# First loads of a decoder layer over two queues, with the other loads behind the first layernorm, and four pieces of work in other places

## The chip, the cores and the metric

One core of one Trainium2 chip runs the kernel. The core has TensorE (PE, matmuls; its weight loads are listed as PEld), VectorE (DVE), ScalarE (ACT), GpSimd (POOL) and SyncE (SP, which here only issues transfers), an on-chip memory of 128 partitions, and matmul accumulators (PSUM) in banks of 512 fp32 numbers a partition. Transfers (DMAs) are issued by SP, ACT or POOL, each on a queue of its own, and carried out by 16 DMA engines. The metric is the device time of one execution in microseconds (us); less is better. All numbers are fp32.

## The reference

A pre-layernorm decoder layer on x (4 batches, 1024 tokens, 512 features), with 16 heads of 32, and a context of 4 x 1024 x 384:

```
def attn(x):                                  # phase 0: gated self-attention
    aperture, expression = sigmoid(x @ Wa + ba), sigmoid(x @ We + be)   # (B, T, 16): the gates
    inner, outer, v = heads(x @ Wi), heads(x @ Wo), heads(x @ Wv)
    a = softmax(inner @ outer.T / sqrt(32)) * aperture[q] * expression[k]
    a = a / (a.sum(-1) + 1e-8)
    c = (a @ v) * sigmoid(iv_p)
    c = rotate(c, angle = pi * sigmoid(beta_p)) * sigmoid(ov_p) * tanh(chi)   # a rotation per head
    return merge(c) @ Wout
def xattn(x, ctx):                            # phase 1: cross-attention
    q, k, v = heads(x @ Wq + bq), heads(ctx @ Wk + bk), heads(ctx @ Wv + bv)
    return merge(softmax(clip(q @ k.T * 32**-0.5)) @ v) @ Wo + bo
def ffn(x):                                   # 64 small networks of 16 hidden units each
    s = x @ Win + bin_                        # (B, T, 64)
    g = (relu(s[..., None] * W1 + b1) * W2).sum(-1) + b2
    return g @ Wout + bout
x = x + attn(layernorm(x)); x = x + xattn(layernorm(x), ctx); return x + ffn(layernorm(x))
```

## The kernel before

**Units of work.** The time is spent in `moderate_path`. There are eight units u: phase 0 (self-attention) for batches 0 to 3, then phase 1 (cross-attention) for batches 0 to 3. A unit has two halves (hf) of 512 query tokens, each half 4 head groups (g) times 8 key tiles (kt), which is 32 steps. A step (`step`, L667) makes the scores of four heads for 128 keys (`scores`: 16 matmul records on PE at L557, two exponentials of 128x1024 on ACT at L562, sums of them on DVE, tile `es`, and in phase 0 `eg`), and then the products with the values of the step before (`times`, L584; L592 for sums of the heads that DVE leaves to PE).

**An order written out by hand.** All five engines are scheduled by hand: each engine runs its instructions in the order in which this program writes them. `pre(u)` holds what a unit needs before its attention: loads of x, layernorm (`ln`, DVE), transposes, projections to k, q and v (all matmuls of a projection are at L87; `evacuate` copies a bank to SBUF, on DVE before the first attention and on ACT after), and in phase 0 the gates (`gates`, `gates_t`). `post(u, hf)` holds what follows: output projection (`o`), layernorm, and in phase 1 the feed-forward: `s` (`inputs`), 17 pieces `h` (`hidden`: one ACT activation and one DVE sum each), `out`. `first` (L1000) runs `pre(0)` and parts of `pre(1)` before the first attention. After that `run(attention(u, hf), beside(u, hf))` deals out the pieces of `beside` among the 32 steps, in proportion to a number of matmul groups that each piece is given; pieces with 0 go along. `weave` mixes two lists evenly. PE has two banks for all this (`bank`, L80).

**Loads.** x0, the first half of batch 0, is one DMA of 1 MB on SP (L134). The rest of `first` goes on SP in order: the key weights Wo in four quarters (`by_quarters`, L89: a quarter is 256 KB, its rows taken as four blocks of 32), the second half of x, Wi and Wv in quarters. ACT issues wae (Wa and We, eight DMAs of 8 KB) and nbae (the gates' biases, eight small DMAs). POOL issues the biases bqk, bvT, bo_bc, bout_bc, the feed-forward's win in quarters, and then, as nothing holds it up, the first 26 DMAs of `load_networks`. A tile framework gives each DMA one of eight semaphores in turn, so a DMA's issue also waits until the one eight DMAs earlier on its kind of queue (SP and ACT together) has landed.

**The gates.** `gates(hf)` multiplies the normalized tokens with wae (L454), takes Exp with nbae on ACT (L460, after `negate` has negated nbae on DVE), adds 1 (tile gi), stores the aperture rows to DRAM (iap_d, L463) and reads them back in another layout (iap, L466). The read-back waits on SP for the four stores. `gates_t(hf)` transposes gi on PE and takes reciprocals on DVE into sw.

**The rotation.** `load_wout` loads Wout, rotj (the rotation's signs) and hp (four numbers a head) late in `first`. `rotations`, the first piece beside the first attention half, computes sigmoids, tanh and the sine and cosine on ACT (Exp, Tanh, Sin) and DVE, and from them four 128x128 matrices rot (L179, L180); `rotate(c)` then multiplies Wout by them on PE, and the product goes to DRAM (wout_d, L190).

**Sums of a head group.** After its eighth key tile a group's sums are copied on ACT (L601, L603, L615), stored to DRAM (`add_up`, L620, L625), read back in another layout (cs, L626, L630), divided on DVE (`divide`, L638) and spread again (L654, L658). DVE comes to `divide` two steps after `add_up`, whether cs has landed or not.

Of the kernel before, what the change touches and what calls it, by code (L numbers as in the profile page):

```python
# [63 lines left out]
def moderate_path(tc: tile.TileContext, a: dict, out: bass.AP, flag: bass.AP):  # L64
    nc = tc.nc
    x = a["x"]
    with ExitStack() as st:
# [21 lines left out]
        def by_quarters(dma, to, w):  # L89

            for c in range(NC):
                dma(to[:, c, :], w.rearrange("(q c i) f -> c q i f", c=NC, i=NB)[c])
# [28 lines left out]
        def load_w(which):  # L121
            w = wp.tile([P, NC, D], F32, tag="w", name="w")
            if which == "o0":
                nc.sync.dma_start(w, wout_d)
            else:
                src, n = W_IN[which]
                if which in ("q0", "k0", "v0", "q1"):
                    by_quarters(nc.sync.dma_start, w, src)
                else:
                    nc.sync.dma_start(w[:, 0:n, :], src.rearrange("(c p) f -> p c f", p=P))  # L130
            return w

        x0 = p2.tile([P, 4, D], F32, tag="inT", name="xin")
        nc.sync.dma_start(x0, x[0].rearrange("(t p) d -> p t d", p=P)[:, 0:4, :])  # L134
        wae = const.tile([P, NC, 2 * H], F32, name="wae")
        by_quarters(nc.scalar.dma_start, wae[:, :, 0:H], a["attn_Wa"])
        by_quarters(nc.scalar.dma_start, wae[:, :, H:], a["attn_We"])

        nbae = const.tile([P, 1], F32, name="nbae")
        for t in range(4):  # L140
            for i, k in enumerate(("attn_ba", "attn_be")):
                nc.scalar.dma_start(nbae[t * 2 * H + i * H : t * 2 * H + (i + 1) * H, :], a[k].unsqueeze(1))
# [8 lines left out]
        def load_wout():  # L151
            raw.append(wp.tile([P, NC, D], F32, tag="w", name="w"))
            nc.sync.dma_start(raw[0], a["attn_Wout"].rearrange("(c p) f -> p c f", p=P))
            nc.sync.dma_start(rotj, a["rotj"])
            nc.sync.dma_start(hp, a["headp"])

        rot = p2.tile([P, NC, P], F32, tag="r2", name="rot")

        def rotations():

            sg = p1.tile([P, 3, NC], F32, name="sg")
            nc.scalar.activation(sg, hp[:, 0:3, :], AF.Exp, scale=-1.0)
            nc.vector.tensor_scalar(sg, sg, 1.0, None, ALU.add)
            nc.vector.reciprocal(sg, sg)
            gain = p1.tile([P, NC], F32, name="gain")
# [8 lines left out]
            cs = p1.tile([P, 2, NC], F32, name="cs")  # L174
            nc.scalar.activation(cs, ang, AF.Sin, scale=math.pi)
# [19 lines left out]
        for k in range(2):  # L195
            nc.gpsimd.dma_start(
                bqk[k * 2 * DH : (k + 1) * 2 * DH], a["bqk"].rearrange("p w (c k) -> p w c k", k=2)[:, :, :, k]
            )

        def broadcast(name, v):  # L200
            t = const.tile([P, D], F32, name=name)
            nc.gpsimd.dma_start(t, v.partition_broadcast(P))
            return t

        bvT = const.tile([P, NC], F32, name="bvT")
        nc.gpsimd.dma_start(bvT, a["xattn_bv"].rearrange("(c p) -> p c", p=P))
        bo_bc = broadcast("bo_bc", a["xattn_bo"])
        bout_bc = broadcast("bout_bc", a["ffn_bout"])
# [17 lines left out]
        by_quarters(nc.gpsimd.dma_start, win, a["ffn_Win"])  # L226
# [112 lines left out]
        def pre(u):  # L339
# [31 lines left out]
            def ln(hf):  # L371
# [11 lines left out]
                def root():  # L383
                    res["rs"] = rsqrt(res["mv"], 4)
# [63 lines left out]
            def gates(hf):  # L448
                def f():
# [19 lines left out]
                    me["gi", hf] = gi  # L469
                return f  # L470

            def gates_t(hf):
                def f():
# [456 lines left out]
        def one(f):  # L930
            return [[(0, f)]]
# [7 lines left out]

        def beside(u, hf):  # L940
# [3 lines left out]
            if u + 1 == n:  # L944
# [7 lines left out]
                out += last["tr"] + weave(last["b"], pause(2)) + last["s"] + weave(last["h"][0:8], pause(14))  # L952
                last["h"] = last["h"][8:]
# [5 lines left out]
            if u + 1 < B:  # L959
                if hf == 0:  # L960
# [3 lines left out]
                    else:  # L964
                        out = one(rotations) + one(fold_bv) + x[1] + k[0][0:1] + [rotate(c) for c in range(NC)]
# [14 lines left out]
            if hf == 0:  # L980
                out = ahead(u + 1, "v") + last["wo"] + p["ctx"][1] + end(k[0] + v[0][0:1]) + last["load"] + v[0][1:2]
                out += last["o"] + weave(last["ln"], v[0][2:])
                if "s" in last:
                    out += last["xT"] + weave(last["b"], k[1][0:2]) + last["tr"] + k[1][2:3] + last["s"] + k[1][3:]
                    held.append(last)
                else:
                    out += k[1]
                return out + xT[0] + v[1][0:2] + tr[0]
# [702 lines left out]
```

## Time and profile before

| | us |
|---|---|
| three runs | 2254.61, 2254.63, 2257.43 |
| median | 2254.63 |
| the profiled execution, its own time | 2255.34 |
| its span in the profile | 2253.5 |
| PE busy | 2192.8 |
| DVE, ACT, POOL busy | 1572.1, 1238.2, 142.9 |
| mean granted clock of PE | 0.994 |
| first matmul (the transposes of x0, L311) | 13.29 |
| first matmul of the key projection | 20.09 |
| first gates' matmul | 40.37 |
| first scores | 113.26 |

The profile is that of one execution, and times inside it count from the span's start. Its own time is the span plus 1.84 us around it. An engine's busy time is the time in which it works on an instruction; waiting and issuing of DMAs are not counted. A row of the timeline has start, length, engine, line, operation, tiles (out<-in), shape and number, and in brackets the idle time of the engine before it and what ended that. SPq, ACTq are the sequencers of SP and ACT, with their DMA issues. The granted clock is that share of TensorE's full clock which it was allowed.

### The profile page before, as it was taken

The page shows a single profiled execution, that of the slowest core. Times are in us where ns is not written, and L with a number is a line of the kernel's source. Part 1 is how long each engine was busy: PE and PEld are TensorE (multiplying, and loading weights), DVE is VectorE, ACT ScalarE, POOL GpSimd, SP SyncE. Part 2 cuts the span into 40 slices and gives each one's busy share as a digit, 9 for nine tenths or more (in the row PEclk, how much of TensorE's full clock was granted, in tenths as well). Part 3 has the DMA queues.
Part 4 walks back from the last instruction along what each step waited for, and adds up shares of the span by engine and source line. Part 5 has one row for each costly group of instructions (what it writes and reads, how often), then busy time and mean ns, then how long its engine had stood idle before and what let it go on. Part 6 is the DMA issues. An engine that isn't in the chain of part 4 may idle for free.

```text
span 2253.5 us, 52768 instructions
## 1 busy us (share of the span) xinstructions
PE 2192.8 (97%) x22590; PEld 552.6 (25%) x22590; DVE 1572.1 (70%) x2498; ACT 1238.2 (55%) x1488; POOL 142.9 (6%) x144
## 2 busy tenths in 40 slices
PE   6999999999999999999999999999999999999995
PEld 2322222222222222222222222222222222222222
DVE  4368776697767957577686666877777776856476
ACT  0055545555455554555656565565756566577673
POOL 4000011000000000000000000101000010101010
PEclk9999999999999999999999999999999999999998
DMA  4422223122231221211413032311223142213131
GB/s 126 108 90 50 69 85 106 36 78 69 87 103 34 80 67 45 80 43 42 118 36 106 26 86 63 109 49 46 74 77 105 44 104 68 58 40 89 47 86 40
DMA packets 153289, 161.71 MB, mean 72 GB/s; under 512 B 46186, under 2 KB 91882, under 8 KB 151892
## 3 DMA queue, kind: packets, MB, share of 16 engines
q1 hardware_dynamic: 149588, 157.19, 24.3%
q8 instruction: 179, 2.93, 0.6%
q0 software_dynamic: 2144, 0.98, 0.3%
q10 hardware_dynamic: 1312, 0.07, 0.1%
q14 instruction: 66, 0.54, 0.1%
HBM read 115.40 MB, written 42.74 MB: 70 GB/s over the span
## 4 chain that ended last, share of the span: by engine, by line
PE 84%; DVE 7%; ACT 4%; DMA 2%; issue 2%; SPq 0%; DVEq 0%; ACTq 0%
PE f L87 32%; PE s L557 22%; PE av L584 18%; PE sm L592 6%; DVE es L570 4%; ACT e L562 3%; PE sm L614 3%; DVE g L847 1%; DMA w<-in_attn_Wo 1%; ACT hid L841 1%; PE f L858 1%; PE f L824 1%; DMA rec_d<-rec 0%; DVE xT L304 0%; DMA wae<-in_attn_Wa 0%
## 5 line engine op out<-in xcount | busy, mean ns | idle before, releaser
L562 ACT ACTIVATE e<-s 128x1024 f32<-128x1024 f32 x1024 | 994.0, 1022 | 730.2 <-PE s L557 541.0
L570 DVE TENSOR_TENSOR es<-es,e 128x1024 f32<-128x1024 f32 x534 | 653.5, 1249 | 274.7 <-ACT e L562 274.0
L557 PE MATMUL s<-q,k 32*64 32x512 f32 x8192 | 626.9, 613 | 11.7 <-ACT e L562 9.6
L584 PE MATMUL av<-e,v 128*32 128x512 f32 x4096 | 554.4, 604 | 0.0
L87 PE MATMUL f<-xT,w 128*32 128x512 f32 x2816 | 331.5, 592 | 0.4 <-PE s L557 0.4
L578 DVE SCALAR_TENSOR_TENSOR eg<-e,sw,eg 128x512 f32<-128x512 f32 x448 | 318.4, 746 | 2.3
L557 PEld LDWEIGHTS s<-q,k 32*64 32x64 f32 x8192 | 137.2, 129 | 470.7 <-ACT e L562 272.5
L568 DVE TENSOR_TENSOR es<-e 128x1024 f32<-128x1024 f32 x89 | 109.6, 1253 | 186.8 <-ACT e L562 175.9
L87 PE MATMUL f<-w,q 128*32 128x512 f32 x1984 | 238.1, 592 | 0.7 <-DVE q L703 0.7
L584 PEld LDWEIGHTS av<-e,v 128*32 128x32 f32 x4096 | 88.4, 108 | 403.7 <-issue 400.8
L87 PEld LDWEIGHTS f<-xT,w 128*32 128x32 f32 x2816 | 93.0, 110 | 211.6 <-issue 203.0
L592 PE MATMUL sm<-e,sw 128*2 128x512 f32 x1024 | 134.0, 595 | 0.0
L761 POOL TENSOR_TENSOR r<-res,bo_bc 128x512 f32<-128x512 f32 x32 | 41.0, 1280 | 1098.8 <-DVE res L753 836.8
L87 PE MATMUL f<-w,xT 128*32 128x512 f32 x896 | 104.6, 592 | 0.6 <-DVE q L270 0.6
L87 PEld LDWEIGHTS f<-w,q 128*32 128x32 f32 x1984 | 66.0, 110 | 149.2 <-issue 142.5
L841 ACT ACTIVATE hid<-sT,units 128x256 f32<-128x256 f32 x128 | 76.0, 603 | 31.9 <-DVE g L847 31.5
L87 PE MATMUL f<-ctxT,w 128*32 128x512 f32 x768 | 92.3, 592 | 0.0
L87 PE MATMUL f<-w,ctxT 128*32 128x512 f32 x768 | 91.9, 592 | 0.0
L614 PE MATMUL sm<-es,ones 128*1 128x512 f32 x348 | 69.0, 591 | 4.2 <-DVE es L570 4.0
L664 DVE TENSOR_TENSOR q<-both,recb 128x512 f32<-128x512 f32 x63 | 46.3, 735 | 27.9 <-DMA recb<-rec_d 27.8
L809 POOL TENSOR_TENSOR res<-res,bout_bc 128x512 f32<-128x512 f32 x28 | 59.6, 2136 | 76.9 <-DVE r L289 76.9
L847 DVE SCALAR_TENSOR_TENSOR g<-hid,units,g 128x256 f32<-128x256 f32 x120 | 57.8, 481 | 8.2 <-ACT hid L841 1.9
(253 smaller groups left out, 1062.9 us busy)
## 6 DMA issues: line engine op xcount, KB each, us to landing
recb<-rec_d SPq DMA_DIRECT2D x252, 64.0 KB
xT<-rows_d SPq DMA_DIRECT2D x60, 256.0 KB
rows_d<-r SPq DMA_DIRECT2D x60, 256.0 KB
w<-in_xattn_Wo SPq DMA_DIRECT2D x9, 1024.0 KB
xin<-in_x SPq DMA_DIRECT2D x8, 1024.0 KB
w<-wout_d SPq DMA_DIRECT2D x8, 1024.0 KB
res<-in_x SPq DMA_DIRECT2D x32, 256.0 KB
x1b_d<-r SPq DMA_DIRECT2D x32, 256.0 KB
```

The costliest lines, as they stand in the source:

```text
L87: nc.tensor.matmul(to[r], lhsT=lhsT[:, j, :] if len(lhsT.shape) == 3 else lhsT[:, r], rhs=rhs, **flags)
L557: nc.tensor.matmul(s[m : m + 64, j, :], lhsT=k[r, g, kt * P + m : kt * P + m + 64], rhs=q[r, g, :], start=True, stop=True,)
L562: nc.scalar.activation(e, s, AF.Exp, scale=SCALE)
L568: nc.vector.tensor_tensor(me["es"][i], me["e", 0][i], es[i], ALU.add)
L570: nc.vector.tensor_tensor(me["es"][i], me["es"][i], es[i], ALU.add)
L578: nc.vector.scalar_tensor_tensor(eg, es[0][:, h, :], gate(kt), eg, ALU.mult, ALU.add)
L584: nc.tensor.matmul(av[r, :], lhsT=me["v"][:, kt, HG * g + h, :], rhs=es[h // 2][:, h % 2, :], start=(kt == 0), stop=(kt == NT - 1),)
L592: nc.tensor.matmul(sm[j * DH : j * DH + sums, :], lhsT=me["sw"][:, t, HG * g + 2 + h, :] if ph == 0 else ones, rhs=me["e", t][1][:, h, :], ...
L614: nc.tensor.matmul(sm[j * DH : j * DH + 1, :], lhsT=ones, rhs=e, start=True, stop=True)
L809: return lambda: nc.gpsimd.tensor_tensor(res[t], res[t], bout_bc, ALU.add)
L841: nc.scalar.activation(hid, res["s"], AF.Relu, bias=units[:, 1, h : h + 1], scale=units[:, 0, h : h + 1])
L847: nc.vector.scalar_tensor_tensor(res["g"], res["hid"], units[:, 2, h - 1 : h], res["g"], ALU.mult, ALU.add)
```

## The change

1. x0 comes in two halves by token blocks, one issued on SP, one on ACT, and Wo's quarters follow in turn on SP, ACT, SP, ACT (`queues`, wk0). `first` no longer loads Wo.
2. Everything else is held until the first layernorm has its reciprocal roots: the load of the second half of x on SP gets a write of four columns by POOL ahead of it, which reads those roots (`me["rs"]`), and SP's DMA waits for that write, since it overwrites it. What stands behind it on SP waits with it: Wi, then wae and nbae (`load_gates`, now on SP), then Wv. POOL's biases and win (`load_biases`) stand behind the same write on POOL, and `load_networks` after them.
3. `rotations` is split. rotj and hp are loaded in `load_rotations`, before Wo of batch 1. `angles` (sigmoids, tanh, sine, cosine) runs before the last query group of batch 0's second half; `rotations` (the four matrices) runs after it, before `gates_t`; both are in `first`, ahead of the first attention.
4. The read-back iap moves from `gates` to `gates_t`, for all batches.
5. Feed-forward: in phase 1 five `h` pieces of a half are woven among the last key and value pieces of the next unit's first half, or three among the last query piece of its second half, with `s` one piece earlier there; `xT[0]` comes before three key pieces. The number of matmuls and of hidden pieces is the same.

```diff
-                dma(to[:, c, :], w.rearrange("(q c i) f -> c q i f", c=NC, i=NB)[c])
+                dma[c % len(dma)](to[:, c, :], w.rearrange("(q c i) f -> c q i f", c=NC, i=NB)[c])
...
-        nc.sync.dma_start(x0, x[0].rearrange("(t p) d -> p t d", p=P)[:, 0:4, :])
+        queues = [nc.sync.dma_start, nc.scalar.dma_start]
+        for i, dma in enumerate(queues):
+            dma(x0[:, 2 * i : 2 * i + 2, :], x[0].rearrange("(t p) d -> p t d", p=P)[:, 2 * i : 2 * i + 2, :])
+        wk0 = wp.tile([P, NC, D], F32, tag="w", name="w")
+        by_quarters(queues, wk0, W_IN["k0"][0])
...
-        by_quarters(nc.scalar.dma_start, wae[:, :, 0:H], a["attn_Wa"])
-        by_quarters(nc.scalar.dma_start, wae[:, :, H:], a["attn_We"])
...
+        def load_gates():
+            by_quarters([nc.sync.dma_start], wae[:, :, 0:H], a["attn_Wa"])
+            by_quarters([nc.sync.dma_start], wae[:, :, H:], a["attn_We"])
+            for t in range(4):
+                for i, k in enumerate(("attn_ba", "attn_be")):
+                    nc.sync.dma_start(nbae[t * 2 * H + i * H : t * 2 * H + (i + 1) * H, :], a[k].unsqueeze(1))
...
+        def load_rotations():
             nc.sync.dma_start(rotj, a["rotj"])
             nc.sync.dma_start(hp, a["headp"])
...
-        def rotations():
+        def angles():
...
             nc.scalar.activation(cs, ang, AF.Sin, scale=math.pi)
+
+        def rotations():
             for i in range(2):
                 nc.vector.tensor_tensor(cs[:, i, :], cs[:, i, :], gain, ALU.mult)
...
+        def load_biases():
...
+            nc.gpsimd.dma_start(bout_bc, a["ffn_bout"].partition_broadcast(P))
+            by_quarters([nc.gpsimd.dma_start], win, a["ffn_Win"])
...
                         xt = p1.tile([P, 4, D], F32, tag="tok", name="xin")
+                        if u == 0:
+
+                            nc.gpsimd.tensor_copy(xt[:, 0, 0:4], me["rs"])
                         nc.sync.dma_start(xt, x[b].rearrange("(t p) d -> p t d", p=P)[:, 4 * hf : 4 * hf + 4, :])
...
+                    me["gi", hf] = gi
+                return f
+
+            def gates_t(hf):
+                def f():
 
                     me["iap", hf] = p4.tile([P, HG, INNER], F32, tag="iap", name="iap")
...
+        def some(half, k):
+
+            h, half["h"] = half["h"][:k], half["h"][k:]
+            return h
...
-                        out = one(rotations) + one(fold_bv) + x[1] + k[0][0:1] + [rotate(c) for c in range(NC)]
+                        out = one(fold_bv) + x[1] + k[0][0:1] + [rotate(c) for c in range(NC)]
...
-                    out += last["xT"] + weave(last["b"], k[1][0:2]) + last["tr"] + k[1][2:3] + last["s"] + k[1][3:]
+                    out += last["xT"] + weave(last["b"], k[1][0:2]) + last["tr"] + k[1][2:3] + last["s"] + xT[0]
                     held.append(last)
...
+                    return out + weave(some(last, 5), k[1][3:] + v[1][0:2]) + tr[0]
...
-                out += last["xT"] + weave(last["b"], q[1][1:3]) + last["tr"] + q[1][3:] + last["s"]
+                out += last["xT"] + weave(last["b"], q[1][1:3]) + last["tr"] + [q[1][3][0:1]] + last["s"]
                 held.append(last)
-                return out
+                return out + weave(some(last, 3), [q[1][3][1:]])
...
-        first = ahead(0, "k") + p["x"][1] + ahead(0, "q") + ahead(0, "v")
-        first += p["x"][0] + p["ln"][0] + p["tr"][0] + p["k"][0] + one(negate) + p["g"][0]
+        S[0]["wk"] = wk0
+        first = p["x"][0] + p["ln"][0] + p["x"][1] + ahead(0, "q") + one(load_gates) + ahead(0, "v") + one(load_biases)
+        first += p["tr"][0] + p["k"][0] + one(negate) + p["g"][0]
...
-        first += p["k"][1] + pres[1]["x"][0] + ahead(1, "k") + p["g"][1]
-        first += weave(pres[1]["ln"][0], p["q"][1]) + pres[1]["xT"][0] + one(load_wout) + p["gt"][1]
+        first += p["k"][1] + pres[1]["x"][0] + one(load_rotations) + ahead(1, "k") + p["g"][1]
+        first += weave(pres[1]["ln"][0], p["q"][1][0:3]) + pres[1]["xT"][0] + one(angles) + p["q"][1][3:]
+        first += one(load_wout) + one(rotations) + p["gt"][1]
```

More of the change, by code (lines that the diff above doesn't have):

```diff
@@ L127, in load_w @@
                 if which in ("q0", "k0", "v0", "q1"):
-                    by_quarters(nc.sync.dma_start, w, src)
+                    by_quarters([nc.sync.dma_start], w, src)
                 else:
@@ L133, in moderate_path @@
         x0 = p2.tile([P, 4, D], F32, tag="inT", name="xin")
-        nc.sync.dma_start(x0, x[0].rearrange("(t p) d -> p t d", p=P)[:, 0:4, :])
+        queues = [nc.sync.dma_start, nc.scalar.dma_start]
[3 more added lines that the diff above has]
+        by_quarters(queues, wk0, W_IN["k0"][0])
         wae = const.tile([P, NC, 2 * H], F32, name="wae")
-        by_quarters(nc.scalar.dma_start, wae[:, :, 0:H], a["attn_Wa"])
-        by_quarters(nc.scalar.dma_start, wae[:, :, H:], a["attn_We"])
         nbae = const.tile([P, 1], F32, name="nbae")
-        for t in range(4):
-            for i, k in enumerate(("attn_ba", "attn_be")):
-                nc.scalar.dma_start(nbae[t * 2 * H + i * H : t * 2 * H + (i + 1) * H, :], a[k].unsqueeze(1))
+        def load_gates():
[4 more added lines that the diff above has]
+                    nc.sync.dma_start(nbae[t * 2 * H + i * H : t * 2 * H + (i + 1) * H, :], a[k].unsqueeze(1))
         def negate():
@@ L153, in load_wout @@
             nc.sync.dma_start(raw[0], a["attn_Wout"].rearrange("(c p) f -> p c f", p=P))
+        rot = p2.tile([P, NC, P], F32, tag="r2", name="rot")
+        cs = p1.tile([P, 2, NC], F32, name="cs")
+        gain = p1.tile([P, NC], F32, name="gain")
+        def load_rotations():
             nc.sync.dma_start(rotj, a["rotj"])
             nc.sync.dma_start(hp, a["headp"])
-        rot = p2.tile([P, NC, P], F32, tag="r2", name="rot")
-        def rotations():
+        def angles():
             sg = p1.tile([P, 3, NC], F32, name="sg")
@@ L164, in rotations @@
             nc.vector.reciprocal(sg, sg)
-            gain = p1.tile([P, NC], F32, name="gain")
             nc.scalar.activation(gain, hp[:, 3, :], AF.Tanh)
@@ L173, in rotations @@
             nc.vector.tensor_tensor(ang[:, 1, :], ang[:, 1, :], sg[:, 0, :], ALU.min)
-            cs = p1.tile([P, 2, NC], F32, name="cs")
             nc.scalar.activation(cs, ang, AF.Sin, scale=math.pi)
+        def rotations():
             for i in range(2):
@@ L194, in moderate_path @@
         bqk = const.tile([P, 2, NC], F32, name="bqk")
[L195 to L203, printed above, removed]
-        bvT = const.tile([P, NC], F32, name="bvT")
-        nc.gpsimd.dma_start(bvT, a["xattn_bv"].rearrange("(c p) -> p c", p=P))
-        bo_bc = broadcast("bo_bc", a["xattn_bo"])
-        bout_bc = broadcast("bout_bc", a["ffn_bout"])
+        bvT = const.tile([P, NC], F32, name="bvT")
+        bo_bc = const.tile([P, D], F32, name="bo_bc")
+        bout_bc = const.tile([P, D], F32, name="bout_bc")
+        def load_biases():
+            for k in range(2):
+                nc.gpsimd.dma_start(
+                    bqk[k * 2 * DH : (k + 1) * 2 * DH], a["bqk"].rearrange("p w (c k) -> p w c k", k=2)[:, :, :, k]
+                )
+            nc.gpsimd.dma_start(bvT, a["xattn_bv"].rearrange("(c p) -> p c", p=P))
+            nc.gpsimd.dma_start(bo_bc, a["xattn_bo"].partition_broadcast(P))
+            nc.gpsimd.dma_start(bout_bc, a["ffn_bout"].partition_broadcast(P))
+            by_quarters([nc.gpsimd.dma_start], win, a["ffn_Win"])
         def fold_bv(part=[]):
@@ L225, in moderate_path @@
         win = const.tile([P, NC, M], F32, name="win")
-        by_quarters(nc.gpsimd.dma_start, win, a["ffn_Win"])
         wout = const.tile([P, D], F32, name="wout")
@@ L383, in root @@
                 def root():
-                    res["rs"] = rsqrt(res["mv"], 4)
+                    res["rs"] = me["rs"] = rsqrt(res["mv"], 4)
                 def norm(t):
@@ L468, in f @@
                     )
[L469 to L473, printed above, removed]
                     tp = bank()
@@ L951, in beside @@
                 out += (ending[0]["load"] if hf else []) + weave(last["ln"], pause(5)) + last["xT"] + pause(8)
-                out += last["tr"] + weave(last["b"], pause(2)) + last["s"] + weave(last["h"][0:8], pause(14))
-                last["h"] = last["h"][8:]
+                out += last["tr"] + weave(last["b"], pause(2)) + last["s"] + weave(some(last, 8), pause(14))
                 held.append(last)
@@ L983, in beside @@
                 if "s" in last:
-                    out += last["xT"] + weave(last["b"], k[1][0:2]) + last["tr"] + k[1][2:3] + last["s"] + k[1][3:]
+                    out += last["xT"] + weave(last["b"], k[1][0:2]) + last["tr"] + k[1][2:3] + last["s"] + xT[0]
                     held.append(last)
-                else:
-                    out += k[1]
-                return out + xT[0] + v[1][0:2] + tr[0]
+                    return out + weave(some(last, 5), k[1][3:] + v[1][0:2]) + tr[0]
+                return out + k[1] + xT[0] + v[1][0:2] + tr[0]
             out = ahead(u + 1, "q") + last["wo"] + end(v[1][2:] + q[0][0:2]) + xT[1]
```

## The prediction

> **What bounds the kernel now.** I read the page first (engines, chain), then the list of what PE waits for, then the chain of waits in order of time for the first 260 us, the busy time in short windows, and the timeline around every place where PE stands still.
>
> ```profile
> PE 2192.8 (97%) x22590; PEld 552.6 (25%) x22590; DVE 1572.1 (70%) x2498; ACT 1238.2 (55%) x1488; POOL 142.9 (6%) x144
> ...
> PE 84%; DVE 7%; ACT 4%; DMA 2%; issue 2%; SPq 0%; DVEq 0%; ACTq 0%
> ```
>
> PE is busy for 97% of the span and no matmul is added or removed. So only PE's idle time (about 53 us) and time at a lower clock can change, and each edit has to be held against one of these waits (engine, line, whom it waited for: us in total, times, longest):
>
> ```profile
> PE f L311 <- DVE xin L289: 13.3, 1, 13.3
> PE s L858 <- DVE g L847: 10.8, 1, 10.8
> PE s L557 <- ACT e L562: 9.6, 23, 1.7
> PE f L87 <- DMA w<-in_attn_Wo: 4.4, 2, 3.6
> PE sm L614 <- DVE es L570: 4.0, 4, 1.2
> ```
>
> The 10.8 is the tail, which the change leaves as it is. The start, from the chain of waits:
>
> ```profile
> 7.05 9.27 DMA w<-in_attn_Wo
> 16.32 0.02 issue
> 16.33 11.12 DMA w<-in_attn_Wo
> 27.45 0.04 issue
> 27.49 13.06 PE f L87 x104
> ```
>
> and from the windows (stretch, us, busy time of PE, PEld, DVE, ACT, POOL, then granted clock, DMA share, GB/s):
>
> ```profile
> 28.00:32.00 4.00, 4.00 (x28) 1.08 (x24) 0.69 (x1) 0.00 (x0) 0.91 (x2) 0.57 0.30 90
> 36.00:40.00 4.00, 4.00 (x44) 1.23 (x40) 0.69 (x1) 0.00 (x0) 0.00 (x0) 1.00 0.26 100
> ```
>
> PE stands until the last quarter of the first key weights lands at 27.45, and then works at clock 0.57 for a while. The second row is a quartered weight alone on the DMA engines: 100 GB/s at a share of 0.26, so four engines of sixteen.
>
> **The change part by part.**
>
> *Start, what goes.* PE loses 0.77 + 3.65 us to the late quarters, and the clock: 104 matmuls took 13.06 us, where the 128 after them took 13.94, which would be 11.33 for 104: 1.73. Together 6.15. The input also comes in two halves on two queues. Now all of it lands at 6.86 and DVE starts at 6.88; its 2 KB packets ran from 1.86 to 5.5, so half are through by 3.7 and would land about 5.0 (the last took 1.3 to land), the rest at 6.3 or 6.4. DVE then does the first two statistics before the second half is there and ends them near 8.0, not at 10.2. Bounds 0 (both halves land together, as late as now) to 2.2; I take 1.5, as the two queues share engines. PE would come to the gates' matmuls at 40.4 - 6.15 - 1.5 = 32.7.
>
> *Start, what is late next.* The gates' weights (wae, 8 DMAs) and biases (nbae, 8) leave ACT's queue, where they landed by 12 and 29, for SP's, behind the second half of x and the four quarters of Wi. Everything with quarters shares four engines. Counted out: x0 off those engines at 5.5; Wo 1.05 MB at 100 GB/s, 10.5, to 16.0; x1 and Wi as before from Wo's last landing (27.45) to Wi's last (41.27), 13.8, with 0.7 to land: 30.5. To this comes POOL's traffic, now released at about 11 and so under x1 and Wi. Before, it held Wo's first packets from the issue at 7.05 to 11.2: bounds 0 to 4.2, I take 3, since it now meets a queue already running. Under the units' small DMAs a quarter of Wo took 3.0 to 3.4 instead of 2.6: 1.5 for four. Then wae: seven of the DMAs took 4.85 to 7.9, or 0.43 each, 3.3 for eight. Sum 38.3, taken as 38. Bounds: without POOL's share 30.5 + 3.3 = 33.8; with Wi at the pace that Wo had in all (7.05 to 27.45, 20.4 us) 16.7 + 3.4 + 20.4 + 3.3 = 43.8, and 51 if x1 also takes the 11.1 that it took (19.71 to 30.83). So PE waits at the gates from 32.7 to 38, 5.3 us; a wait of 3.65 brought the low clock, so I charge 1.7 again. Net: 40.4 - 38 - 1.7 = 0.7 gained; ends +6.6 and -5 (-12 in the last case).
> The biases come 2 us after wae, near 40. Behind them stand DVE's negation, the gates' Exp with its table load (1.28 + 0.37), and the bank that PE's second query group needs: 41.8, while PE gets there at 42.3 or later. Cover 0.5; beyond it each us costs one. Wv is issued after them, at 39 to 40, lands 10.5 later, before PE wants it (53).
> The Trainium skill speaks against the two queues: "DMA: Bandwidth & Descriptors", Rules for kernel authors, says that queues of different issuers share the same sixteen DMA engines and interleave, so spreading adds no bandwidth. The row at 100 GB/s has one queue only and cannot show it. If two queues did double Wo's rate, all behind it would come 5.2 earlier and the start would gain about 6 instead of 0.7; by the rule it stays at 0.7. I go by the unchanged rate of the row.
>
> *Angles.* Before, ACT loads the tables for Sin and for Exp again between the first scores (start us, us, what):
>
> ```profile
> 116.56 1.28 ACT L175 ACT_TABLE_LOAD   x1
> 118.08 1.28 ACT L562 ACT_TABLE_LOAD   x1
> 120.45 2.00 PE L557 MATMUL s<-q,k 32*64 32x512 f32 x16 [1.75 <-ACT e L562]
> ```
>
> The angles now run among the last query groups, where ACT is idle for 29 us; the reload of Exp stands ahead of ACT's wait for the scores, so it is covered by that idle time (uncovered: 1.28). Gone: 1.75, and 0.37 at 114.37, where the next batch's blocks were late; they are loaded earlier now. Added ahead of the gates' reciprocal: DVE's ten rotation operations, 2.4 us. The bank is free 0.69 + 2.4 + 0.55 = 3.7 after the query matmuls, and PE wants it after 0.75 + 3.43 = 4.2: covered by 0.5. Rotj and headp go past Wo of batch 1, 72 KB: nothing waits. Gain 2.1; bounds 0 to 2.3.
>
> *The gates' reload (iap).* On SP it waited for the gates' rows, which lie behind Wv on the four engines, and the sums of the first heads stood behind it:
>
> ```profile
> 159.84 0.38 SPq L466 DMA_DIRECT2D iap<-iap_d  x1
> 160.33 0.53 SPq L620 DMA_DIRECT2D sum_d<-both  x1
> 166.04 0.19 DVE L638 TENSOR_TENSOR both__1314<-cs 128x32 f32<-128x32 f32 x1 [6.76 <-DMA cs<-sum_d]
> 170.79 1.22 PE L557 MATMUL s<-q,k 32*64 32x512 f32 x8 [1.40 <-ACT e L562]
> ```
>
> The sums were ready at 152.4. DVE stood still until 166.04 and PE lost 1.40; then the clock is at half for 3.41 us from 171.62, another 1.7. Without the reload the sums still share engines with Wv, whose quarters land at 150.2, 153.1, 156.4 and 159.0, and the issue waits for those landings; the read-back goes out near 160 instead of 162.46 and lands near 163.5 instead of 165.9. That is 2.4 earlier, more than the 1.40: wait and clock both go. Gain 3.1; bounds 0 to 3.1. The later reloads end no wait of PE, so they are worth 0; moved past the rows' stores, each reload is still far ahead of its use in the next attention half.
>
> *Feed-forward.* ACT's hidden units (0.60 each; DVE's sums 0.48) come three or five earlier, so 14 and 12 instead of 17 are left for the start of the next half. Waits there: 0.74 + 0.32 + 0.74 (1477 to 1491; again near 1740) and 1.15 (1606 to 1627; again near 1875), 5.9 in all.
>
> ```profile
> 1477.92 2.00 PE L557 MATMUL s<-q,k 32*64 32x512 f32 x16 [0.74 <-ACT e L562]
> ```
>
> In the built order of ACT the steps with four pieces besides the exponentials, which cost the 0.74, remain; those with three become two. But the last step of three halves now gets a copy and three units. Bounds +2.3 (all of the 1.15s) to -2.2 (three more of 0.74); I take 0.
>
> *Sum.* 0.7 + 2.1 + 3.1 + 0 = 5.9. The profiled execution took 2255.34 (span 2253.5 and 1.84 around it), which gives 2249.4. It stood 0.71 above the median of the three runs, 2254.63; so 2248.7 for the median. A difference under 0.2% (4.5 us) can't be told from none here.
>
> **The rivals.**
> *The gates' weights come in time.* POOL's traffic does not hold the four engines: wae at 33.8 to 34.5, a wait too short for the clock: start +6, sum 11.2, 2243.4. For it: Wo's quarters took 2.6 each once POOL was quiet. Against: POOL's 24 small DMAs now run from 20 to 40.
> *The gates' weights come much later.* SP's queue is one line: x1, Wi, wae, nbae. If x1 and Wi are held as x1 and Wo were (11.1 and 20.4), wae lands at 51, the start loses 12 and the other 5.2 don't pay for it: 2261. The sign turns when wae lands after 44, and it is 0.2% slower after 48. For it: those two durations. Against: then ACT's sixteen small DMAs and the semaphores shared with them lay in between.
> *One of the moves buys nothing* (the sums still behind Wv, or the units' four-piece steps cost as much as was saved): 3 less, 2251.7, no change to be measured.
>
> **How the numbers follow.** Forecast 0.42, in time 0.19, buys nothing 0.28, much later 0.11. The forecast's own range is 2246 to 2251. The range asked for goes from the first rival to well past the third, 2243 to 2255; the far end of the late case is left out. Faster by over 0.2% (below 2250.1): most of the forecast, 0.37, and 0.19: 0.56. Within: 0.05 + 0.28 = 0.33. Slower: 0.11.
>
> **What would show it.** Right: first matmuls of the projection without a wait for Wo, near 18.6; a wait at the gates' matmuls for wae, ended near 38, then a clock below 1 for 3 to 5 us; no table load between the first exponentials; no wait near 165, no half clock after it. Wrong: no wait at the gates (first rival), a query or value projection that waits for Wi or Wv, DVE held at the negation past 42, or PE's waits near the ends of the feed-forward halves up by more than 2 us.

## The result, and the profile after

The changed kernel takes 2247.09 us (median of six runs, 2244.28 to 2253.92; six runs of the kernel before on the same chip: 2255.04, 2254.29 to 2259.63). The ratio is 0.9964, 95% interval 0.9948 to 0.9979: faster by 0.36%. The profiled execution took 2244.28 us, the lowest of the six, with a span of 2242.5 (before: 2253.5). So the forecast of 2248.7 is close, and the sign is right. Term by term it is not: two terms were about right, the start went the wrong way, and the largest gain came from the edit that was costed at nothing.

The page of the changed kernel, its busy times and the shares of its chain of waits:

```profile
PE 2185.6 (97%) x22590; PEld 552.0 (25%) x22590; DVE 1569.7 (70%) x2498; ACT 1238.0 (55%) x1488; POOL 143.5 (6%) x145
...
PE 85%; DVE 6%; ACT 3%; issue 2%; DMA 2%; SPq 1%; DVEq 0%; ACTq 0%; POOL 0%
```

PE has the same 22590 matmuls and is busy 7.2 us less. That is the first sign that its busy time held something that could go. The list of what PE waits for (us in total, times, longest):

```profile
PE f L321 <- DVE xin L299: 11.8, 1, 11.8
PE s L871 <- DVE g L860: 10.8, 1, 10.8
PE f L467 <- DMA wae<-in_attn_We: 8.5, 1, 8.5
PE s L570 <- ACT e L575: 5.4, 18, 1.0
```

The wait for Wo is gone, the first layernorm is 1.5 us shorter, the tail is the same, and one wait of 8.5 us for the gates' weights is new. The timeline there (start, length, engine, line, operation, idle time before it):

```profile
40.28 1.94 PE L467 MATMUL f<-xin,wae 128*32 128x128 f32 x32 [8.47 <-DMA wae<-in_attn_We]
...
44.92 0.15 DVE L152 TENSOR_SCALAR nbae<-nbae 128x1 f32<-128x1 f32 x1 [12.36 <-DMA nbae<-in_attn_be]
45.15 1.28 ACT L473 ACT_TABLE_LOAD   x1 [45.15 <-DVE nbae L152]
```

PE comes to the gates at 40.28 - 8.47 = 31.81 and stands until 40.28; the granted clock is at half for 10.24 us from 35.21. The biases are ready for the negation only at 44.92. The windows before that (length, busy time of PE, PEld, DVE, ACT, POOL, granted clock, DMA share, GB/s):

```profile
6.00:12.00 6.00, 0.19 (x5) 0.22 (x9) 5.41 (x22) 0.00 (x0) 0.81 (x2) 1.00 0.26 101
...
20.00:24.00 4.00, 4.00 (x44) 1.27 (x40) 0.69 (x1) 0.00 (x0) 2.73 (x6) 1.00 0.63 152
24.00:28.00 4.00, 4.00 (x44) 1.20 (x40) 0.69 (x1) 0.00 (x0) 3.23 (x6) 1.00 0.35 73
36.00:40.00 4.00, 0.00 (x0) 0.00 (x0) 0.00 (x0) 0.00 (x0) 3.66 (x7) 0.50 0.30 40
```

From 6 to 12 us Wo comes over two queues, all but alone (the held loads are issued from 11.3 on), at 101 GB/s and a share of 0.26: the same rate that one queue had before. From 20 to 28 POOL issues its loads (busy 2.7 and 3.2 of 4 us), and the quarters behind them crawl.

Where the 11.0 us between the two profiled executions lie is best seen from the starts of the scores, as each step has the same 16 score matmuls in both and, apart from the moved pieces, the same work beside them. The table has the time of the first scores, the time between the first scores of two steps, and phase 1 (from its first scores, step 256, to the end of the span). Step 0 is the first of batch 0. The experiments stand below the two kernels. The first six columns of numbers are of one profiled execution each. Experiments 1 to 4, 5 to 8 and 9 to 12 ran on three different chips, so each ratio is to runs of the kernel before on the same chip (medians 2256.64, 2256.18 and 2255.01).

| | first scores | steps 0-4 | 4-16 | 16-256 | phase 1 | span | median | ratio to before, 95% |
|---|---|---|---|---|---|---|---|---|
| before | 113.26 | 16.46 | 51.06 | 1034.64 | 1038.05 | 2253.5 | 2255.04 | |
| changed | 115.59 | 14.39 | 46.96 | 1035.23 | 1030.29 | 2242.5 | 2247.09 | 0.9948-0.9979 |
| 1: before, four unit buffers | 114.77 | 16.45 | 48.76 | 1035.11 | 1019.39 | 2234.5 | 2238.37 | 0.9905-0.9933 |
| 2: feed-forward as before | 114.90 | 14.39 | 46.96 | 1036.09 | 1038.24 | 2250.6 | 2252.84 | 0.9978-0.9996 |
| 3: loads as before | 114.25 | 14.39 | 47.16 | 1037.28 | 1030.51 | 2243.6 | 2245.37 | 0.9942-0.9969 |
| 4: POOL late | 114.18 | 14.39 | 46.96 | 1035.19 | 1032.96 | 2243.7 | 2248.07 | 0.9948-0.9976 |
| 5: changed, four unit buffers | 115.52 | 14.39 | 46.96 | 1034.96 | 1020.98 | 2232.8 | 2234.72 | 0.9896-0.9923 |
| 6: reload as before | 116.31 | 15.11 | 50.96 | 1034.95 | 1032.91 | 2250.2 | 2252.09 | 0.9970-0.9988 |
| 7: gates on ACT, POOL late | 110.07 | 14.39 | 46.96 | 1035.85 | 1033.57 | 2240.8 | 2242.62 | 0.9933-0.9960 |
| 8: one queue | 116.12 | 14.39 | 46.96 | 1035.20 | 1030.53 | 2243.2 | 2249.39 | 0.9962-0.9984 |
| 9: before, three unit buffers | 112.67 | 19.54 | 48.84 | 1035.23 | 1022.10 | 2238.4 | 2239.15 | 0.9913-0.9945 |
| 10: angles as before | 114.73 | 19.70 | 46.96 | 1035.80 | 1033.64 | 2250.8 | 2251.62 | 0.9969-0.9991 |
| 11: 7 and four buffers | 109.96 | 14.39 | 46.99 | 1037.86 | 1020.21 | 2229.4 | 2231.15 | 0.9871-0.9907 |
| 12: 11, feed-forward as before | 109.75 | 14.39 | 46.96 | 1035.93 | 1020.05 | 2227.1 | 2231.43 | 0.9874-0.9910 |

The change itself: start -2.33, steps 0 to 4 +2.07, steps 4 to 16 +4.10, then -0.59 up to phase 1 (1034.6 to 1037.9 in all the profiles, so no more than their spread), and +7.76 in phase 1: 11.0 us. The attention's start and the first sums look as the prediction said they would: no table load stands between the exponentials, and DVE comes to the first division earlier and after a shorter wait.

```profile
118.49 1.33 PE L570 MATMUL s<-q,k 32*64 32x512 f32 x16
119.64 1.94 ACT L575 ACTIVATE e<-s 128x1024 f32<-128x1024 f32 x2 [0.96 <-PE s L570]
...
159.59 0.67 SPq L639 DMA_DIRECT2D cs<-sum_d  x1
163.14 0.19 DVE L651 TENSOR_TENSOR both__1314<-cs 128x32 f32<-128x32 f32 x1 [3.60 <-DMA cs<-sum_d]
```

ACT now waits for PE's scores there, not PE for ACT. The division came at 166.04 after 6.76 us of idle time, and comes at 163.14 after 3.60.

### The profile page after: what moved, and what is told of

It reads as the page before. It is cut to its first block, busy times and chain, and to the rows that moved or that the text cites. A ratio compares the mean times of both kernels' runs of the same rounds, so it can differ in the third digit from the quotient of the medians.

```text
span 2242.5 us, 52755 instructions
## 1 busy us (share of the span) xinstructions
PE 2185.6 (97%) x22590; PEld 552.0 (25%) x22590; DVE 1569.7 (70%) x2498; ACT 1238.0 (55%) x1488; POOL 143.5 (6%) x145
## 4 chain that ended last, share of the span: by engine, by line
PE 85%; DVE 6%; ACT 3%; issue 2%; DMA 2%; SPq 1%; DVEq 0%; ACTq 0%; POOL 0%
PE f L87 32%; PE s L570 23%; PE av L597 19%; PE sm L605 6%; DVE es L583 3%; PE sm L627 3%; ACT e L575 2%; SPq L92 1%; DVE g L860 1%; PE f L871 1%; PE f L837 1%; ACT hid L854 1%; DMA sum_d<-both 1%; DMA rec_d<-rec 0%; DVE xT L314 0%
```

## The experiments

**Why the feed-forward gained (1, 9, 2, 5).** In phase 1 the steps that became shorter are those at a half's start in which ACT has two or three hidden units. One such step of the kernel before, from its timeline:

```profile
1601.94 2.36 DVE L570 TENSOR_TENSOR es<-es,e 128x1024 f32<-128x1024 f32 x2 [0.92 <-ACT e L562]
...
1602.71 0.60 ACT L841 ACTIVATE hid<-sT,units 128x256 f32<-128x256 f32 x1
...
1604.22 1.07 DVE L847 SCALAR_TENSOR_TENSOR g<-hid,units,g 128x256 f32<-128x256 f32 x2
...
1604.80 0.60 ACT L841 ACTIVATE hid<-sT,units 128x256 f32<-128x256 f32 x1 [1.49 <-DVE g L847]
...
1606.85 2.00 PE L557 MATMUL s<-q,k 32*64 32x512 f32 x16 [0.18 <-ACT e L562]
```

The tile `hid` has two buffers. The second unit of a step overwrites the buffer that DVE's sum in the piece before it must read first; that sum stands on DVE behind the two sums `es` of the step (2.36 us), and these behind the step's exponentials. So ACT stands for 1.49 us, the copy and the next exponentials come late, and PE's scores get their two accumulators one after the other: the 16 matmuls take 2.00 us and not 1.11. Only 0.18 of it is listed as idle time. Neither ACT nor DVE is full in that stretch. The edit that tests it, on the kernel before alone:

```diff
-                        hid = p2.tile([P, 2 * P], F32, tag="hid", name="hid")
+                        hid = p2.tile([P, 2 * P], F32, tag="hid" if h % 4 < 2 else "sw", name="hid")
```

> The kernel before with one edit: the feed-forward's hidden units get four buffers in turn instead of two (h 2 and 3 of each four lie in the two buffers that phase 0 uses for its gates sw). Nothing is moved. Theory A (a loop over two buffers: the unit after next on ACT overwrites a buffer that DVE has yet to read, DVE stands behind the two sums of the step, these behind the step's second exponential, so ACT stands still 1.48 us in each step with two or more units, and the next step's exponentials with it): ACT's waits for g (31.5 us in 28 waits) nearly go, the steps of the second halves of batches 1 and 2 that take 4.62, 4.63, 4.92, 4.97 and 4.64 us fall towards 3.76 to 4.3, and the kernel gains at least what the change gained there, 7.5 to 10 us, of the kernel before. Theory B (ACT simply has too much to do in these steps, two exponentials, three units and a copy): the steps stay within 0.2 us of their length and the gain is 0 to 1 us.

Measured: 2238.37 us, ratio 0.9919 (0.9905 to 0.9933), 18.3 below the kernel before, with nothing moved; the changed kernel's ratio is 0.9964. Phase 1 is 18.66 shorter, about twice what was expected as a floor: theory A, and more of it, as the first halves have such steps too (the two halves of batch 1 are 4.2 and 5.7 us shorter, those of batch 2 4.2 and 5.2). The same step and the next in this kernel's timeline:

```profile
1597.09 1.10 ACT L841 ACTIVATE hid<-sT,units 128x256 f32<-128x256 f32 x2
...
1600.70 1.58 ACT L841 ACTIVATE hid<-sT,units 128x256 f32<-128x256 f32 x3
1601.48 1.11 PE L557 MATMUL s<-q,k 32*64 32x512 f32 x16
```

Two units, and then three, run without a gap, and the scores take 1.11. The steps that took 4.63, 4.92, 4.97 and 4.64 us take 3.76 each. Four such steps in one window of the kernel before, and then of the first experiment (length, busy PE, PEld, DVE, ACT, POOL, clock, DMA share, GB/s):

```profile
1602.22:1621.39 19.17, 18.53 (x165) 4.36 (x161) 14.41 (x22) 13.23 (x20) 0.00 (x0) 1.00 0.05 16
```

```profile
1597.70:1612.80 15.10, 15.10 (x172) 3.69 (x168) 14.37 (x22) 13.19 (x20) 0.00 (x0) 1.00 0.08 20
```

DVE and ACT have the same 22 and 20 instructions and the same busy time, and PE the same matmuls in the four steps (the windows' ends cut a few more or fewer off the next). Yet the stretch is 4.07 us shorter, and of these the kernel before shows only 19.17 - 18.53 = 0.64 as idle time of PE. The rest was "busy": while one accumulator is not free, four score matmuls run side by side where eight do in the first experiment (their starts in the trace come in fours, 0.43 to 0.48 us apart, in the row of 2.00 us, and in eights, 0.48 apart, in the row of 1.11), and both count as busy.

Three buffers test the dose:

```diff
+                        hid = p2.tile([P, 2 * P], F32, tag="hid" if h % 3 < 2 else "sw", name="hid")
```

> The kernel before with three buffers for the hidden units instead of two (every third unit in the two that phase 0 uses). Theory of the loop: a unit then waits for the sum two pieces before it, so the second unit of a step no longer waits for DVE and the third still does: steps of the second halves of batches 1 and 2 with two units (4.63 and 4.64 us with two buffers) fall to 3.76, those with three (4.92, 4.97) stay above 4.1; ACT's waits for g lie between 3.3 us (four buffers) and 31.5 (two); phase 1 is 9 to 15 us shorter than before, where four buffers gave 18.7. If the number of units in a step costs by ACT's time alone, three buffers differ from two by less than 1 us, and if any extra buffer removes the whole loop, by 18.7.

Measured: 2239.15 us (ratio 0.9929), phase 1 15.95 us shorter, a little over the expected 9 to 15 and short of 18.66. ACT's waits for g, from the lists of waits of the kernel before, of three buffers and of four:

```profile
ACT hid L841 <- DVE g L847: 31.5, 28, 2.7
```

```profile
ACT hid L841 <- DVE g L847: 8.3, 8, 2.7
```

```profile
ACT hid L841 <- DVE g L847: 3.3, 2, 2.3
```

The order is as the loop says. One part of the expectation missed: the steps with three units fell to 3.76 and 3.91, not to something over 4.1. The third unit does still wait there (1.15 us at 1604.59), but only the step after it is longer, by 0.15. In the first halves one such step stays long: 5.25 us, between 5.50 with two buffers and 4.72 with four.

The feed-forward's pieces back in their old places, in the changed kernel:

```diff
-                    out += last["xT"] + ... + last["s"] + xT[0]
+                    out += last["xT"] + ... + last["s"] + k[1][3:]
...
-                    return out + weave(some(last, 5), k[1][3:] + v[1][0:2]) + tr[0]
...
-                return out + weave(some(last, 3), [q[1][3][1:]])
```

> The changed kernel with the feed-forward's pieces where they were (all 17 hidden units left for the start of the next half, inputs after the last key or query piece). Theory of the traces (the feed-forward's pieces brought the gain from step 324 on): 7.5 to 8.5 us slower than the changed kernel, so within 3 to 4 us of the kernel before. The prediction's step (what the pieces save at the start of a half is given back at the end of the one before): the same as the changed kernel within 1 us.

Measured: phase 1 1038.24, so the whole gain there is gone (7.95 us); the median is 2252.84, 3.8 below the kernel before on the same chip. The moved pieces brought the gain. And the change with four buffers:

> The changed kernel with four buffers in turn for the hidden units, the same edit as in the first experiment. Theory A (two buffers made a loop of ACT and DVE; the change gained in phase 1 only by having fewer units in those steps): phase 1 becomes as short as in the kernel before with four buffers, so from step 324 to the end within 2 us of that kernel's, 8 to 11 us shorter than in the changed kernel; in all 2235 to 2239. Rival (the moved pieces bring something of their own, as the steps' work is more even): phase 1 ends 3 us or more ahead of the first experiment's.

Measured: 2234.72 us (0.9909), phase 1 1020.98 against 1019.39 without the move. With the loop gone, moving the pieces is worth nothing in phase 1: it had helped only by taking units out of the steps in which they waited.

**The start (3, 4, 7, 8).** The loads as before, with the other edits kept (x0 as one load on SP, wae and nbae on ACT, no write by POOL, Wo behind x0):

> The changed kernel with all first loads as in the kernel before (x0 as one load on SP, gates' weights and biases on ACT, POOL's loads without a wait, Wo behind x0 on SP); angles, reload and feed-forward stay changed. Theory of the traces: first scores at 113.3 instead of 115.6, so 2.3 us faster than the changed kernel, with the waits of 0.77 and 3.65 us for Wo back and the wait for wae gone. The prediction's step: 0.7 us slower than the changed kernel. If the moved angles cost something in the start, the first scores come later than 113.3 by that.

Measured: first scores at 114.25, 1.3 earlier than in the changed kernel's profile, not 2.3. Both starts spread by more than I had allowed, since the clock falls to half after the wait for spells of 3.41, 6.83 or 10.24 us. The same loads gave 113.26, 114.77 and 112.67 (before, 1 and 9: mean 113.57), the held loads 115.59, 114.90, 115.52, 116.31 and 114.73 (changed, 2, 5, 6, 10: mean 115.41). So the held loads lose some 1.8 us (1.7 with this experiment's own 114.25), from one profile of each kernel; the medians (2245.37 here) can't show that.

POOL's loads released later, by a second small copy:

```diff
         def load_biases():
+            nc.gpsimd.tensor_copy(bo_bc[:, 0:4], S[0]["q", 0][:, 0, 0:4])
...
-        first = ... + one(load_gates) + ahead(0, "v") + one(load_biases)
+        first = ... + one(load_gates) + ahead(0, "v")
...
-        first += weave(p["ln"][1], p["q"][0]) + p["gt"][0]
+        first += weave(p["ln"][1], p["q"][0]) + one(load_biases) + p["gt"][0]
```

> The changed kernel with POOL's biases, win and networks released only after the first query projection's first copy, by one more small copy on POOL; nothing else. Theory A (POOL's loads hold the four engines that carry the quarters, from 16 to 28 us): Wi's last quarter lands at 33 to 35 instead of 38.3, the wait for wae at the gates falls from 8.5 to 3 to 5 us, and the first scores come 3.5 to 5 us earlier than 115.6. Theory B (x1 and Wi are late by their own doing, x1 beside Wo's last quarters and SP's issues waiting for landings eight loads back): wae lands at 40 or later as now, and the first scores stay within 1 us of 115.6.

Measured, in its list of PE's waits and a window:

```profile
PE f L87 <- DVE xT L315: 3.0, 1, 3.0
...
PE f L87 <- ACT gi L474: 1.6, 1, 1.6
...
PE f L87 <- DMA w<-in_attn_Wv: 0.6, 1, 0.6
PE f L468 <- DMA wae<-in_attn_We: 0.2, 1, 0.2
...
24.00:28.00 4.00, 4.00 (x44) 1.22 (x40) 0.69 (x1) 0.00 (x0) 0.00 (x0) 1.00 0.28 105
```

Theory A holds for the loads: 105 GB/s in the window where the changed kernel has 73, Wi's last quarter at 31.6 and not 38.3, and the wait for wae falls from 8.5 to 0.2. The expected gain failed all the same: the first scores are at 114.18, 1.2 before the mean. PE came earlier to the next late things, ACT's gates behind nbae (1.61), Wv (0.62) and the second half of x, which comes back from DRAM for the second key projection (3.02, then half clock for 3.41).

So the seventh experiment also took wae and nbae out of the line:

```diff
-                    nc.sync.dma_start(nbae[...], a[k].unsqueeze(1))
+                    nc.scalar.dma_start(nbae[...], a[k].unsqueeze(1))
...
-        first = p["x"][0] + p["ln"][0] + p["x"][1] + ahead(0, "q") + one(load_gates) + ahead(0, "v")
+        first = one(load_gates) + p["x"][0] + p["ln"][0] + p["x"][1] + ahead(0, "q") + ahead(0, "v")
```

> The changed kernel with POOL's loads late as in the fourth experiment, and with the gates' weights and biases on ACT's queue behind Wo's two quarters, held by nothing. Theory (the start lost because wae and nbae stood at the end of one line that POOL's loads slowed): no wait for wae, none for ACT's gi, Wi lands at 31 to 33; first scores 5 to 9 us earlier than 115.6, at 107 to 110. Rival (another wait takes the place: the second half of x, written to DRAM and read back for the second key projection, which cost 3.0 us at 66 in the fourth experiment): that wait grows by what PE comes earlier, and the first scores stay at 112 or later.

Measured: first scores at 110.07, 5.3 before the mean of the held loads and 3.5 before that of the old ones; 2242.62 us. The timeline at the gates:

```profile
29.70 3.19 PE L87 MATMUL f<-xin,w 128*32 128x512 f32 x28
32.70 1.06 PE L468 MATMUL f<-xin,wae 128*32 128x128 f32 x32
33.70 2.78 PE L87 MATMUL f<-xin,w 128*32 128x512 f32 x24
36.77 11.37 PE L87 MATMUL f<-xin,w 128*32 128x512 f32 x104 [0.29 <-DMA w<-in_attn_Wi]
```

No wait at the gates and no half clock. Wi came later than expected (its last quarter at 36.7, not at 31 to 33, as SP's second half of x was issued at 17.48 only, behind a landing of wae), but at PE's pace. The rival's wait for x stayed at 2.77 and did not grow. Experiments 11 and 12, with the same start, have their first scores at 109.96 and 109.75. The gates' weights on ACT's queue without the later release of POOL's loads were not run, so the two edits' shares are known only from this order.

One queue for x0's halves and Wo:

```diff
-        queues = [nc.sync.dma_start, nc.scalar.dma_start]
+        queues = [nc.sync.dma_start, nc.sync.dma_start]
```

> The changed kernel with x0's two halves and Wo's four quarters all on SP's queue; the rest held as before. Theory (the quarters share four engines whatever queue issues them, 100 GB/s by one queue or two): Wo's last quarter lands within 1 us of 18.8, the key projection still waits for no Wo, the first transposes come 0 to 1 us later than 11.8, and the first scores lie within 1.5 us of 115.6. Rival (the second queue brings bandwidth): Wo's last quarter lands 4 us or more later, PE waits for it 2 us or more.

Measured: Wo's last quarter at 20.6 instead of 18.8, PE waits 0.43 for it, first scores at 116.12. In the window where Wo is alone:

```profile
6.00:10.00 4.00, 0.00 (x0) 0.00 (x0) 3.52 (x17) 0.00 (x0) 0.00 (x0) 1.00 0.26 99
```

99 GB/s by one queue, 101 by two, and the first scores within the expected 1.5 us. Three details missed: the last quarter is 1.8 us later and not within 1, PE does wait for it, and the first transposes come at 10.69, 1.1 us earlier than with two queues and not later. On one queue x0's halves land one after the other (4.3 and 5.6), on two together (5.4 and 5.9). As the layernorm ended earlier, the held loads were released 1.1 us earlier too (POOL's first at 10.20 instead of 11.32), so the 1.8 us may be theirs and not the queue's.

**The two small moves (6, 10).** The reload in the gates again:

```diff
                         nc.sync.dma_start(iap_d[b][hf][:, ts(t, P)], gi[t * 2 * H : t * 2 * H + H, :])
+                    me["iap", hf] = p4.tile([P, HG, INNER], F32, tag="iap", name="iap")
+                    nc.sync.dma_start(me["iap", hf], iap_d[b][hf].rearrange(...))
```

> The changed kernel with the read-back iap issued in the gates again, ahead of the sums' transfers on SP; nothing else. Theory (the read-back on SP held up the first sums): DVE comes to the first division of cs at 165 to 166 instead of 163.1, PE waits 1 to 1.5 us for ACT's exponentials near 169 and the clock is at half for 3.4 us after it; between steps 4 and 16, 3 to 4.1 us are lost. Rival (the gain between these steps came from the earlier start of the changed kernel's batch 0 and from the loads' order): the same as the changed kernel within 0.5 us.

Measured: steps 4 to 16 take 50.96 instead of 46.96, 4.0 us, all of it in step 14 (8.62 instead of 4.62); the wait for ACT is 1.30 and half clock follows for 3.41. The reload stands ahead of the sums on SP again:

```profile
161.86 0.38 SPq L478 DMA_DIRECT2D iap<-iap_d  x1
162.34 0.53 SPq L633 DMA_DIRECT2D sum_d<-both  x1
...
167.65 0.19 DVE L651 TENSOR_TENSOR both__1316<-cs 128x32 f32<-128x32 f32 x1 [6.66 <-DMA cs<-sum_d]
...
172.40 1.71 PE L570 MATMUL s<-q,k 32*64 32x512 f32 x8 [1.30 <-ACT e L575]
```

The division comes later than the expected 165 to 166, as this execution's first scores are 0.7 later (116.31) and another 0.7 is lost in steps 0 to 4, where PE waits 0.66 for the next batch's blocks. The angles back beside the first attention half (loads after Wout, work ahead of `fold_bv`):

```diff
-        first += weave(pres[1]["ln"][0], p["q"][1][0:3]) + pres[1]["xT"][0] + one(angles) + p["q"][1][3:]
+        first += weave(pres[1]["ln"][0], p["q"][1]) + pres[1]["xT"][0]
...
-                        out = one(fold_bv) + x[1] + k[0][0:1] + ...
+                        out = one(angles) + one(rotations) + one(fold_bv) + x[1] + k[0][0:1] + ...
```

> The changed kernel with rotj, headp, the angles and the rotation matrices where they were (loads after Wout, work beside the first attention half); nothing else. Theory (the table loads for Sin and Exp stood between the first exponentials): the wait of 1.3 to 1.8 us for ACT near step 1 is back, and 1.7 to 2.3 us are lost between the first scores and step 4; the first scores come within 0.5 us of the changed kernel's apart from the start's own spread of some 1 us. Rival (the gain at the first steps came from blocks and loads that are ready earlier): lost less than 0.6 us.

Measured: the table loads and the wait are back,

```profile
118.03 1.28 ACT L185 ACT_TABLE_LOAD   x1
119.55 1.28 ACT L575 ACT_TABLE_LOAD   x1
121.92 2.04 PE L570 MATMUL s<-q,k 32*64 32x512 f32 x12 [1.97 <-ACT e L575]
```

and steps 0 to 4 take 19.70, which is 5.3 more and not 2: the clock was at half for 6.83 us after the wait of 1.97. In the ninth experiment, with the angles in the same place, it was so too (19.54); in the kernel before and the first it was not (16.46, 16.45).

**Together (11, 12).** The start of the seventh, the four buffers of the fifth, and in the twelfth the feed-forward's old places:

> The changed kernel with the start of the seventh experiment and the four buffers of the fifth. If the two gains lie in places that do not touch each other, they add: first scores at 110 +- 1, phase 1 at 1021 us as in the fifth, in all 4 to 5.5 us below the fifth, so 2229 to 2231. If the earlier start meets another wait in phase 0, less than 3 us below the fifth.

> As the eleventh, but with the feed-forward's pieces where the kernel before has them. Theory (with four buffers there is no loop that the moved pieces could shorten, and the three units beside a copy in a half's last step cost a little): 0.5 to 2 us faster than the eleventh, phase 1 at 1019.4 instead of 1021. Rival (the moved pieces even out ACT's work): 1 us or more slower than the eleventh.

Measured: 2231.15 and 2231.43 us, ratios 0.9889 (0.9871 to 0.9907) and 0.9892 (0.9874 to 0.9910). The eleventh is 3.6 us below the fifth on the median (on another chip, and the intervals overlap), a little less than forecast. In the places of the two gains the profiles add up: first scores 5.6 earlier (109.96), phase 1 0.8 shorter (1020.21). But 2.9 are lost between steps 16 and 256 (1037.86 against 1034.96), where a new wait of 1.84 stands at 202; its cause is open, and the twelfth doesn't have it (1035.93). The twelfth is the same as the eleventh within what can be told, not 0.5 to 2 us faster as expected, and phase 1 is the same to 0.2 us: with four buffers the moved pieces cost and bring nothing that shows. Both beat the kernel before by some 24 us, where the change brought 8.

## Why the prediction came out so near, and where it was wrong

*What bounds the kernel.* "So only PE's idle time (about 53 us) and time at a lower clock can change" is the step that failed. Phase 1 of the first experiment is 18.66 us shorter with the same matmuls. In all, the kernel before and the first experiment differ by 53.3 - 47.4 = 5.9 us of idle time ahead of PE's matmuls, and by 2192.8 - 2179.8 = 13.0 us of PE's busy time. A wait that halves the number of matmuls side by side is no idle time. I read the idle gaps and never compared the lengths of steps that have the same matmuls; 3.76 beside 4.92 stood in the trace, and so did ACT's wait of 31.5 us for g.

*Feed-forward*, costed at 0 with bounds from +2.3 to -2.2. The gain was 7.76 in the profiles of the two kernels. Both bounds were built from PE's idle gaps of 5.9 us, so the truth lay outside. What I feared at the halves' last steps (a copy and three units) is real: there is a new wait of 1.00 at 1711.73, and in four of the other profiles with the moved pieces and two buffers (4, 6, 7, 10) a wait of 1.30 at the second such place, with phase 1 at 1032.9 to 1033.6. So the edit is worth 4.4 to 7.8 us from one execution to the next.

*Start*, predicted +0.7, measured -2.33 in the profile and some -1.8 on the mean. What goes was right: no wait for Wo, and 1.48 instead of 1.5 at the first transposes, though not for the reason given (the halves landed together, earlier than the whole had). The mis-sized term is the sum that ends with wae landing at 38.3: PE was let go at 40.28, and the last of the eight landed at 41.4. The sum has Wi's last quarter at 30.5 without POOL's traffic and 4.5 more with it (the 3 and the 1.5); it landed at 38.3, and at 31.6 where POOL's loads came late. So POOL's loads cost 6.7 and not 4.5, and the rest of the count was 1.1 short. The biases, taken as near 40 with a cover of 0.5, let DVE go at 44.92; no wait of PE is listed for them, as the low clock had PE late as well, but where PE came on time they cost 1.61.

*The rule on queues.* The prediction weighed what the Trainium skill says in "DMA: Bandwidth & Descriptors", Rules for kernel authors: spreading transfers over issuers brings no bandwidth. The runs agree for this shape: 99 GB/s by one queue, 101 by two. The last quarter came 1.8 us earlier with two, but there the held loads came 1.1 us later too, so this doesn't speak for the second queue.

*Angles*, predicted 2.1: 2.07. The price is 5.3 where the clock falls, which I had not charged here though a wait of 1.40 brought it elsewhere.

*Reload*, predicted 3.1 (1.40 and 1.7): 4.10, and 4.0 by undoing it. The mechanism held, and all of it lies in step 14: 8.72 us before, 4.62 changed. Experiments 1 and 9, with the old reload, have waits of 0.74 and 0.82 us for ACT there and no half clock after them, and the step takes 6.42 and 6.50. So the reload is worth 1.8 where the clock holds and 4.1 where it falls, and of the 1.8 only 0.74 is listed as idle time, so here too the idle time shows less than the loss.

*Why the total was near.* Of the profiled difference of 11.0, 5.9 had been predicted; the start missed by -3.0, reload and feed-forward by +1.0 and +7.8, and the stretch up to phase 1 by -0.6. The median shows less than the profile (8.0), as the changed kernel's profiled execution was its best. That the total came within 1.6 us of the forecast is luck: errors of opposite sign, the largest of them bigger than the whole forecast gain of 5.9. The rival in which the gates' weights come much later had the right direction for the start, not the size; nothing in my list held the cause of the gain.

## What to carry to other kernels

Where steps repeat the same matmuls, compare their lengths before trusting the idle time of a "97% busy" engine, and look for the engine that waits inside the longer ones. A ring of two buffers between two engines that work in order is a loop as soon as two of its pieces fall into one step: add buffers before moving work. When loads are put in a line behind an event, ask what each arrival finds next, since removing one wait only brings the next late thing forward.

## What was not expected of the hardware

PE's records call it busy at half its use: 16 score matmuls take 1.11 us when both accumulators are free and 2.00 when they come one after the other, and the second case shows 0.2 us of idle time. The spells of half clock last 3.41, 6.83 or 10.24 us, multiples of one length (the last one, in the tail, is cut off by the end), and which of them follows a wait can't be told from its length: none after 1.32, 1.75 and 2.77 us, 3.41 after 1.40 and 3.02, 3.41 after 1.30 in experiments 4 and 6 but none after 1.30 in 7 and 10, 6.83 after 1.97, and after the 7 to 9 us at the gates 6.83 or 10.24. The Trainium skill ("TensorE: Matmul & The Clock Gate", What's actually happening) gives the window in which the clock gate counts as free-running and 3413 ns long (4096 cycles of the half clock); the lengths of one, two and three such windows agree with it. So the wait at the first steps was worth 2.1 us in some executions (1.32 and 1.75 long) and 5.2 or 5.3 in others (1.97).
